# Sums of the left weights bound behind the evictions of block 0's self stage

## The chip, the cores and the metric

The kernel runs on one core of one Trainium2 chip. The metric is device time in microseconds (us) of one execution, as the median of several runs. A profiled execution of the same program gives the trace from which every other duration here is read. Engines: PE is TensorE (PEld its weight loads), DVE is VectorE, ACT is ScalarE, POOL is GpSimd, SP is SyncE; SPq and POOLq are their DMA issues.

## What is computed

Two layers over x (128 sequences of 64 tokens, 768 features, f32), cut here to what matters:

```python
# layer 0
u = h @ h.T / sqrt(d);  p = softmax(u);  attn = (p * adj) / (sum(p * adj) + 1e-10)
h_left, h_self, h_right = h @ W_left.T + b_left, h @ W_self.T + b_self, h @ W_right.T + b_right
ctx = upper(attn) @ h_left + diag(attn) * h_self + lower(attn) @ h_right
x = layernorm(x + relu(layernorm(ctx) * gamma + beta))
# layer 1: 12 heads, scores + beta * adj, masked where adj is 0
x = layernorm(x + softmax(mask(q @ k.T / 8 + beta * adj)) @ v)      # q, k, v = x @ W + b
```

The three weight matrices W_self, W_left and W_right of layer 0 are what this case is about, and of those the work of the first 128 us or so.

## The kernel before, in words

The 8192 tokens are worked in 16 blocks of 512 (four tiles of 128). Every large product of a block, 512 tokens by a 768 x 768 matrix, is made by a scheme with seven products of halves in place of eight (`seven`, L365). For it the weight matrix W is cut into quarters b00, b10, b01, b11 (128 x 1152 each, loaded by SP), and from them four sums are formed on DVE, in this order: t5 = b01 - b00, t6 = b11 - t5, then b01 = b11 - b01 in place (factor 7), and t4 = b10 - t6 (`prepare`, L198; the list of steps is its `later(...)` call). The block's transposed tokens hT are treated in the same way on POOL (`combined`, L312).

`seven` walks the products in the order 1, 2, 6, 5, 7, 4, 3, each for j = 0 and j = 1, that is 14 products of six matmuls (128 x 384). Products 1, 6, 7, 4 add up in one PSUM bank X[j]; 2 and 3 stand in others: 2 in Y[j], then 5 and 3 together in a fresh Y[j]. DVE reads the bank out between them, and PE may go on in it only when DVE has read it:

- after product 1, u1 = X + bias (`first`, L413 to L415)
- after product 2, o = Y + u1 (`last` of `self_part`, L589 to L591), which frees Y for product 5
- after product 6, u2 = X + bias; product 7 for the same j comes on top in X and so waits for that
- after product 7, u3 = X + bias, and o = Y + u3 from what product 5 left; product 4 comes on top in X and waits for u3, and product 3 on top in Y
- after product 4 and after product 3, the last two parts of o.

Block 0 does its self stage (`self_part(0, ...)`, L978), its left stage (L982) and its right stage (L988) with weights that have just been formed in SBUF. Each sum is also stored to DRAM (`store`, L218), so that later blocks stream it. The pieces of the left matrix are asked for by `prepare("l", wst, prep, (2, 1, 0))` at L976: quarters in pieces of 128 x 384 from the pool `wst`, so that each of its sums is three DVE instructions (L234) in place of one; its three new tiles t5, t6, t4 stand in the pool `prep`, which has seven slots, all in use by the self matrix at first. The right matrix's quarters take `prep` slots as those of the self matrix come free, so SP's issues of them wait for PE.

What sets the order: in this part of the program a scheduler lays each engine's instructions in order by its own estimate of when they can start; after that an engine takes them strictly in that order. `prepare` puts the sums in the queue `lazy`, and `step` (L137), called after each product of `seven`, takes from the queues what is due, which settles where they are traced. `tc.issue_after(ins)` adds an ordering edge, with no wait of its own at run time: the instructions traced in its block come after `ins` in the order of the engine of `ins`. `recent["u"]` holds the last DVE eviction that was traced. From block 1's stages on `recent["bound"]` is set (L995) and `step` traces everything behind `recent["u"]`; for block 0 it isn't, and there only the sum 7 of the self matrix is bound (L243).

Of the kernel before, what the change touches and what calls it, by code (L numbers as in the profile page):

```python
# [51 lines left out]
def gnn_two_layers(ctx: ExitStack, tc, x, adj, wl, bl, ws, bs, wr, br, gamma, beta,  # L52
# [52 lines left out]
    for half, sign in ((0, 1), (1, -1)):  # L105
        for g in range(2):
            nc.gpsimd.affine_select(
                out=side[half * L : (half + 1) * L, g, :], in_=side[half * L : (half + 1) * L, g, :],
# [12 lines left out]
    def later(key, *fs, queue=lazy):  # L121
        queue.extend((key, f) if callable(f) else (key, *f) for f in fs)
# [12 lines left out]
    recent = {}  # L135
# [45 lines left out]
    def chunks(pool, name):  # L181


        if pool is not wst:
            tile_ = pool.tile([P, HC, HALF], F32, tag="w", name=name)
            return [tile_[:, k, :] for k in range(HC)], tile_
        return [wst.tile([P, HALF], F32, tag="w", name=name) for _ in range(HC)], None

    def move(queue, whole, parts, to=None, source=None):

        if whole is not None:
            queue.dma_start(out=whole if source is not None else to, in_=source if source is not None else whole)
        else:
            for k in range(HC):
                queue.dma_start(out=parts[k] if source is not None else to[:, k, :],
                                in_=source[:, k, :] if source is not None else parts[k])

    def prepare(nm, quarter_pool, sum_pool, waits=(0, 0, 0), queue=lazy):  # L198

        w = weights[nm].rearrange("(p c) e -> p c e", c=KC)
        src = {(0, 0): w[:, 0:HC, 0:HALF], (0, 1): w[:, 0:HC, HALF:D],
               (1, 0): w[:, HC:KC, 0:HALF], (1, 1): w[:, HC:KC, HALF:D]}
        b = {}
        for q in ((0, 0), (1, 0), (0, 1), (1, 1)):
            b[q] = chunks(quarter_pool, f"b{q[0]}{q[1]}_{nm}")

            with tc.issue_after(streamed["l"][8]) if nm == "k" else ExitStack():
                move(nc.sync, b[q][1], b[q][0], source=src[q])  # L210
        t5, t6, t4 = (chunks(sum_pool, f"t{i}_{nm}") for i in (5, 6, 4))
        in_sbuf = {1: b[0, 0], 2: b[1, 0], 3: b[1, 1], 5: t5, 6: t6, 7: b[0, 1], 4: t4}
        key = ("w", nm)
        if nm in "slrv":
            d = tc.dram_tile([4, P, HC, HALF], F32, name=f"d_{nm}")
            pieces[nm] = {1: src[0, 0], 2: src[1, 0], 3: src[1, 1], 5: d[0], 6: d[1], 7: d[2], 4: d[3]}

        def store(i):  # L218
            if nm in "slrv":
                if i in (5, 6, 7, 4):  # L220
                    move(nc.gpsimd, in_sbuf[i][1], in_sbuf[i][0], to=pieces[nm][i])
            else:


                engine, first = (nc.sync, streamed["s"][20]) if nm == "q" else (nc.gpsimd, last_sum[1].ins)
                with tc.issue_after(first):
                    for hg in range(NHG):
                        engine.dma_start(out=qk_d[hg, i - 1, :, "qk".index(nm)],
                                        in_=in_sbuf[i][1][:, :, hg * P : (hg + 1) * P])

        def formed(i, out, left, right):
            if any(a[1] is None for a in (out, left, right)):
                for k in range(HC):
                    nc.vector.tensor_tensor(out[0][k], left[0][k], right[0][k], ALU.subtract)  # L234
            else:
                nc.vector.tensor_tensor(out[1], left[1], right[1], ALU.subtract)
            store(i)

        def idle():
            pass  # L240

        def formed7():
            with tc.issue_after(evicted["s"].ins) if nm == "s" else ExitStack():  # L243
                formed(7, b[0, 1], b[1, 1], b[0, 1])


        later(key, *[idle] * waits[0], partial(formed, 5, t5, b[0, 1], b[0, 0]),
              *[idle] * waits[1], partial(formed, 6, t6, b[1, 1], t5), formed7,
              *[idle] * waits[2], partial(formed, 4, t4, b[1, 0], t6), queue=queue)
        if nm in "qk":  # L250
            later(key, lambda: store(1), lambda: store(2), lambda: store(3), queue=queue)
        return {i: a[0] for i, a in in_sbuf.items()}
# [771 lines left out]
    for n in range(NBLK):  # L1024
        m, p = n + 1, n - 1
        left, right, own, val = {}, {}, {}, {}
# [174 lines left out]
```

## Time and profile before

| what | value |
|---|---|
| runs shown | 2936.67, 2934.70, 2934.53 us; median 2934.7 |
| profiled execution, its own time | 2938.14 us |
| its span in the trace | 2936.4 us, mean granted PE clock 0.995 |
| PE busy | 2879.9 us, 98% of the span |
| DVE busy | 1989.5 us, 68% |
| ACT, POOL busy | 1123.6 us (38%), 729.9 us (25%) |
| DMA over the span | 210 GB/s |
| block 0's self stage, first to last weight load | 16.19 to 49.36 us |
| block 0's left stage, first weight load | 49.36 us |

In a timeline a row has the start in us, the duration in us, the engine, the line of the kernel, the operation, what it writes and reads, and, in square brackets, how long the engine had sat idle before it and what ended that. A row with x3 stands for three instructions that follow each other. In a table by stretches each row has the bounds of the stretch, its length, the busy time of PE, PEld, DVE, ACT and POOL in it with the number of instructions, the granted PE clock (1.00 is full speed), the DMA share and the rate.

### The profile page before, as it was taken

The page shows a single profiled execution, that of the slowest core. Times are in us where ns is not written, and L with a number is a line of the kernel's source. Part 1 is how long each engine was busy: PE and PEld are TensorE (multiplying, and loading weights), DVE is VectorE, ACT ScalarE, POOL GpSimd, SP SyncE. Part 2 cuts the span into 40 slices and gives each one's busy share as a digit, 9 for nine tenths or more (in the row PEclk, how much of TensorE's full clock was granted, in tenths as well). Part 3 has the DMA queues.
Part 4 walks back from the last instruction along what each step waited for, and adds up shares of the span by engine and source line. Part 5 has one row for each costly group of instructions (what it writes and reads, how often), then busy time and mean ns, then how long its engine had stood idle before and what let it go on. Part 6 is the DMA issues. An engine that isn't in the chain of part 4 may idle for free.

```text
span 2936.4 us, 49944 instructions
## 1 busy us (share of the span) xinstructions
PE 2879.9 (98%) x17578; PEld 1935.1 (66%) x17578; DVE 1989.5 (68%) x4034; ACT 1123.6 (38%) x2114; POOL 729.9 (25%) x879
## 2 busy tenths in 40 slices
PE   8999999999999999999999999999999999999997
PEld 5657567585665856658576575766757567585685
DVE  5678677676676766667667576666767667676656
ACT  0004324354243543434444344443434424354254
POOL 3133122304132130411405124051230413313110
PEclk9999999999999999999999999999999999999998
DMA  9788786849578595775958759486694966849442
GB/s 322 221 274 276 234 233 194 249 138 290 154 197 248 144 285 152 214 231 163 271 147 239 203 175 271 135 260 183 185 260 137 282 163 198 244 139 287 140 127 90
DMA packets 440278, 613.18 MB, mean 209 GB/s; under 512 B 53584, under 2 KB 416720, under 8 KB 440032
## 3 DMA queue, kind: packets, MB, share of 16 engines
q1 hardware_dynamic: 362096, 493.57, 56.0%
q10 hardware_dynamic: 60848, 44.05, 8.2%
q0 software_dynamic: 17088, 72.37, 6.7%
q8 instruction: 143, 2.34, 0.3%
q14 instruction: 103, 0.84, 0.1%
HBM read 539.43 MB, written 77.27 MB: 210 GB/s over the span
## 4 chain that ended last, share of the span: by engine, by line
PE 91%; ACT 3%; POOL 2%; DVE 2%; DMA 1%; issue 1%; SPq 0%; ACTq 0%; DVEq 0%
PE ps_X L384 35%; PE ps_Y L384 26%; PE ps_Y L638 11%; PE ps_X L638 10%; PE ps_ctx L677 3%; ACT eT L853 2%; PE sc L835 2%; PE ps_y L882 2%; PE u L527 2%; POOL q L337 1%; ACT L853 1%; ACT uqk L804 1%; POOL q L336 0%; PE ps_x L286 0%; DVE o L892 0%
## 5 line engine op out<-in xcount | busy, mean ns | idle before, releaser
L384 PE MATMUL ps_X<-xT,wqk 128*128 128x256 f32 x1728 | 395.9, 381 | 9.6 <-ACT uqk L804 9.6
L853 ACT ACTIVATE eT<-s 32x256 f32<-32x256 f32 x768 | 317.8, 414 | 184.7 <-DVE s L862 174.6
L384 PEld LDWEIGHTS ps_X<-xT,wqk 128*128 128x128 f32 x1728 | 325.8, 190 | 67.1 <-ACT uqk L804 16.2
L317 POOL TENSOR_TENSOR S<-hT 128x768 f32<-128x768 f32 x16 | 28.9, 1808 | 1133.4 <-PE ps_Y L384 1102.2
L384 PE MATMUL ps_Y<-S,wqk 128*128 128x256 f32 x1152 | 264.3, 379 | 0.0
L682 ACT ACTIVATE unused<-o 128x768 f32<-128x768 f32 x60 | 50.6, 843 | 500.4 <-DVE o L679 304.9
L384 PEld LDWEIGHTS ps_Y<-S,wqk 128*128 128x128 f32 x1152 | 218.9, 190 | 29.8
L438 DVE TENSOR_TENSOR lr<-ps_Y,u_deep 128x384 f32<-128x384 f32 x273 | 152.1, 557 | 108.6 <-PE ps_Y L638 82.8
L638 PE MATMUL ps_Y<-wlr,q 128*128 128x384 f32 x546 | 208.6, 491 | 0.0
L384 PE MATMUL ps_X<-wv,xT 128*128 128x384 f32 x576 | 195.0, 489 | 0.0
L804 ACT ACTIVATE uqk<-ps_X,bq 128x256 f32<-128x256 f32 x144 | 68.3, 474 | 324.9 <-PE ps_X L384 323.7
L812 DVE TENSOR_TENSOR q<-ps_Y,uqk 128x256 f32<-128x256 f32 x144 | 61.0, 424 | 177.7 <-ACT uqk L804 89.4
L384 PE MATMUL ps_X<-ws,hT 128*128 128x384 f32 x540 | 179.4, 486 | 0.1
L892 DVE SCALAR_TENSOR_TENSOR o<-ps_y,rz,o 128x64 f32<-128x64 f32 x768 | 165.0, 277 | 6.8
L638 PE MATMUL ps_X<-wlr,q 128*128 128x384 f32 x364 | 151.1, 497 | 14.5 <-POOL q L337 5.9
L384 PEld LDWEIGHTS ps_X<-wv,xT 128*128 128x128 f32 x576 | 108.2, 190 | 80.8 <-issue 8.4
L438 DVE TENSOR_TENSOR u_deep<-ps_X,lr 128x384 f32<-128x384 f32 x195 | 107.3, 550 | 68.0 <-PE ps_X L638 66.4
L384 PEld LDWEIGHTS ps_X<-ws,hT 128*128 128x128 f32 x540 | 102.4, 190 | 71.8 <-DMA ws<-in_L_gnn_W_self_dram 0.7
L638 PEld LDWEIGHTS ps_Y<-wlr,q 128*128 128x128 f32 x546 | 101.6, 190 | 67.2
L415 DVE TENSOR_TENSOR u<-ps_X,bv 128x384 f32<-128x384 f32 x96 | 53.4, 556 | 130.3 <-PE ps_X L384 130.2
L384 PE MATMUL ps_X<-S,wqk 128*128 128x256 f32 x576 | 138.2, 385 | 0.0
L384 PE MATMUL ps_Y<-xT,wqk 128*128 128x256 f32 x576 | 135.6, 385 | 0.0
(247 smaller groups left out, 5482.6 us busy)
## 6 DMA issues: line engine op xcount, KB each, us to landing
wlr<-lr_d SPq DMA_DIRECT2D x819, 192.0 KB, 3.5
wqk<-qk_d SPq DMA_DIRECT2D x672, 192.0 KB, 2.4
wv<-d_v SPq DMA_DIRECT2D x192, 192.0 KB, 3.3
ws<-d_s SPq DMA_DIRECT2D x180, 192.0 KB, 6.0
wv<-in_L_gnn_Wv_dram SPq DMA_DIRECT2D x144, 192.0 KB, 4.1
ws<-in_L_gnn_W_self_dram SPq DMA_DIRECT2D x135, 192.0 KB, 5.5
xa<-in_x_dram SPq DMA_DIRECT2D x64, 384.0 KB, 5.4
out_dram<-o POOLq DMA_DIRECT2D x62, 384.0 KB, 6.2
```

The costliest lines, as they stand in the source:

```text
L384: nc.tensor.matmul(ps, lhsT=a, rhs=b, start=(c == 0 and i in (1, 2, 5)), stop=(c == len(fs) - 1), skip_group_check=True)
L415: recent["u"] = evicted[nm] = nc.vector.tensor_tensor(u, ps, bias[nm][:, b * HALF : (b + 1) * HALF], ALU.add)
L438: nc.vector.tensor_tensor(dst, view(ps), add, ALU.add)
L527: nc.tensor.matmul(u[g * L : (g + 1) * L, t, :], lhsT=xT[:, c, tok], rhs=xT[:, c, tok], start=(c == 0), stop=(c == KC - 1))
L638: nc.tensor.matmul(ps, lhsT=a, rhs=b, start=(k == 0 and j in (1, 2, 5)), stop=(k == len(fs) - 1), skip_group_check=True)
L677: nc.tensor.matmul(ps[g * L : (g + 1) * L, 0:HALF], lhsT=blk["aT"][:, t, g * L : (g + 1) * L], rhs=blk["lr"][t][:, g, cols], start=True, s ...
L804: nc.scalar.activation(u, ps, AF.Identity, bias=bias["qk"[j]][:, c : c + 1])
L812: nc.vector.tensor_tensor(dst, ps, part, ALU.add)
L835: nc.tensor.matmul(sc[r][g * L : (g + 1) * L, t, c, :], lhsT=q[rows, c, tok], rhs=k[rows, c, tok], start=True, stop=True)
L853: nc.scalar.activation(e[cols, :, rows], pairs[rows, :, cols], AF.Exp)
L882: nc.tensor.matmul(y[r, h][cols, t, c, :], lhsT=eT[rows, 2 * h + t, c, cols], rhs=v[rows, 2 * h + t, g, hg + c * HC, :], start=True, stop= ...
L892: nc.vector.scalar_tensor_tensor(res[:, r, c, hg, :], ps[:, t, k, 0:HD], rz[:, t, k : k + 1], res[:, r, c, hg, :], ALU.mult, ALU.add)
```

## The change

The DVE subtractions of `formed` move into a function `subtracted`, and for the left matrix alone they are traced behind the eviction that was traced last. The store stays outside the bound block. The self, right and layer 1 matrices are traced as before.

```diff
         def formed(i, out, left, right):
+
+            with tc.issue_after(recent["u"].ins) if nm == "l" else ExitStack():
+                subtracted(out, left, right)
+            store(i)
+
+        def subtracted(out, left, right):
             if any(a[1] is None for a in (out, left, right)):
                 for k in range(HC):
                     nc.vector.tensor_tensor(out[0][k], left[0][k], right[0][k], ALU.subtract)
             else:
                 nc.vector.tensor_tensor(out[1], left[1], right[1], ALU.subtract)
-            store(i)
```

Lines of the kernel below L239 stand five lines further down in the changed kernel.

In the built programs, DVE's order between the eviction of product 6, j = 0, and the first evictions of the left stage goes from this (evictions named by their product; t and b are the left sums)

```
before: ev6/0  t5 t5 t5 t6  ev6/1  t6 t6 b b b t4 t4 t4  ev7/0 o  ev7/1 o  ev4/0  ev4/1  ev3/0  (t_r)  ev3/1
after:  ev6/0  ev6/1  ev7/0 o  ev7/1 o  t5 t5 t5  ev4/0  ev4/1  t6 t6 t6  ev3/0  b b b  ev3/1  t4 t4 t4
```

and the right sums (t_r) move behind the left stage's evictions of products 1 and 2. PE's, ACT's and POOL's orders are the same in both. In SP's order the first load of a quarter of W_right moves behind two small loads (bv, adj), and the first two loads for W_v move ahead of some of the six loads of W_self for block 1; from the load of d_s on it is the same.

## The prediction

> **What bounds the kernel now.** I read the busy shares and the slices of the page first. PE is busy for 98% of the span, so elsewhere an edit on DVE is worth nothing; what can be won lies where PE stands or is slow.
>
> ```profile
> PE 2879.9 (98%) x17578; PEld 1935.1 (66%) x17578; DVE 1989.5 (68%) x4034; ACT 1123.6 (38%) x2114; POOL 729.9 (25%) x879
> PE   8999999999999999999999999999999999999997
> ```
>
> Then PE's waits. One DVE eviction (L415) costs PE 2.9 us in one piece, the second longest PE wait in the list; the longest, 5.5 us, is the load of x at the start.
>
> ```profile
> PE ps_x L286 <- DMA xa<-in_x_dram: 6.8, 2, 5.5
> PE ps_X L384 <- DVE u L415: 2.9, 1, 2.9
> ```
>
> The timeline places it in block 0's self stage. I read it against the products: the PE row at 31.78 is product 7 (both j), the one at 38.82 is product 4, the one at 45.81 product 3, the one at 49.68 product 1 of the left stage.
>
> ```profile
> 29.25 0.55 DVE L415 TENSOR_TENSOR u<-ps_X,bs 128x384 f32<-128x384 f32 x1
> 29.72 1.49 DVE L234 TENSOR_TENSOR t_l<-b_l 128x384 f32<-128x384 f32 x3
> 31.78 4.14 PE L384 MATMUL ps_X<-b_s,hT 128*128 128x384 f32 x12
> 32.63 0.56 DVE L234 TENSOR_TENSOR t_l<-b_l,t_l 128x384 f32<-128x384 f32 x1 [1.43 <-DMA b_l<-in_L_gnn_W_left_dram]
> 33.11 0.55 DVE L415 TENSOR_TENSOR u<-ps_X,bs 128x384 f32<-128x384 f32 x1
> 34.46 1.03 DVE L234 TENSOR_TENSOR t_l<-b_l,t_l 128x384 f32<-128x384 f32 x2 [0.80 <-DMA b_l<-in_L_gnn_W_left_dram]
> 35.40 1.49 DVE L234 TENSOR_TENSOR b_l<-b_l 128x384 f32<-128x384 f32 x3
> 36.81 1.49 DVE L234 TENSOR_TENSOR t_l<-b_l,t_l 128x384 f32<-128x384 f32 x3
> 38.22 0.55 DVE L415 TENSOR_TENSOR u<-ps_X,bs 128x384 f32<-128x384 f32 x1
> 38.82 7.16 PE L384 MATMUL ps_X<-t_s,hT 128*128 128x384 f32 x12 [2.90 <-DVE u L415]
> 45.81 4.03 PE L384 MATMUL ps_Y<-b_s,S 128*128 128x384 f32 x12
> 49.68 4.03 PE L384 MATMUL ps_X<-b_l,hT 128*128 128x384 f32 x12
> ```
>
> Twelve sums of left weights stand in DVE's queue ahead of the eviction of product 7 (38.22), two of them waiting for loads of W_left. Product 7, j = 0, had ended near 33.7, so its eviction is over 4 us late, and PE stands. And then product 4 takes 7.16 us where every other such row takes 4.03. The table by stretches of 3.41 us (the clock is the third number from the end) shows why:
>
> ```profile
> 34.72:38.13 3.41, 1.20 (x4) 0.38 (x2) 3.41 (x8) 0.00 (x0) 2.14 (x4) 1.00 0.96 370
> 38.13:41.54 3.41, 2.72 (x5) 1.51 (x6) 2.21 (x5) 0.00 (x0) 0.54 (x1) 0.50 1.01 362
> 41.54:44.96 3.42, 3.42 (x7) 1.91 (x6) 0.56 (x1) 0.00 (x0) 0.00 (x0) 0.50 1.04 412
> 44.96:48.37 3.41, 3.41 (x11) 1.98 (x11) 0.98 (x2) 0.00 (x0) 1.48 (x2) 1.00 1.05 377
> ```
>
> The clock is halved from 38.13 to 44.96.
>
> **What the Trainium skill says.** "TensorE: Matmul & The Clock Gate", Part 1 (The HAM clock gate): the PE clock goes to half after an idle window of about 3413 ns and back after a busy one, and the windows run free, not from the kernel's start. The trace agrees: 44.96 - 38.13 = 6.83 us is two such windows. It adds that a window need not be all idle: that from 34.72 was 35% busy (1.20 of 3.41) and halved the clock, and the next, 80% busy, did not restore it. "Perfetto Trace Analysis", Tensor Engine Instruction: DVE takes its queue strictly in order; the trace agrees, the eviction at 38.22 starts as the last sum ends.
>
> **The change, part by part.**
>
> 1. *The two late evictions are freed.* No instruction is added or removed; the ordering edge is inside one engine and waits for nothing at run time. By the changed order DVE goes from the eviction at 29.25 straight to that of product 6, j = 1 (29.72 to 30.3; its product ended near 27.9). Product 7, j = 1, thus no longer waits, and PE keeps its pace of 3.87 us per product (weight loads start at 23.72, 27.59, 31.46). Product 7, j = 0, starts at 31.78 and ends at 33.7; DVE starts about 0.2 us later (the trace: product 3 starts at 45.81, takes 1.94 for j = 0, evicted at 47.95), so 33.9, done 34.5. Product 4 needs this at 31.78 + 3.87 = 35.65: 1.2 us early. Then o (35.06), and product 7, j = 1: 35.86 to 36.4, needed at 37.6.
>
> 2. *The stall goes*: product 4 at 35.65 in place of 38.82, that is 3.17 us.
>
> 3. *The slow clock goes with it*: product 4 took 45.81 - 38.82 = 6.99 us of PE's time where 3.87 is its pace, 3.12 us. Without an idle window it isn't slowed. Sum in the profiled execution: 6.29 us, the left stage's first weight load from 49.36 to 31.46 + 3 x 3.87 = 43.07.
>
> 4. *The sums in their new place.* t5 after the two o: 37.0 to 38.4 (three at 0.47 each); the loads that DVE waited for had landed by 34.46. Evictions of product 4 at 38.4 and 39.7; t6 40.3 to 41.7; eviction of product 3 to 42.2; b to 43.6; eviction to 44.15; t4 to 45.6. Left product 1 ends its j = 0 at 45.3, so its eviction (45.6 to 46.1) starts just behind the last sum, five us before product 6 needs it. Left product 6 needs t6 at 43.4 + 2 x 3.87 = 51.1: nine us in hand. Cost nothing, hidden by products 4 and 3 of the self stage; were the sums nine us later, PE would stand in the left stage instead.
>
> 5. *The right sums* follow the left stage's evictions of products 2. SP issues the quarters of W_right as prep slots come free: the third at 46.01 and the fourth at 49.88 now, as products 4 and 3 end; then at about 39.6 and 43.5. The third landed by 52.73, 6.7 us after issue; the rows of these loads go from 4.3 to 14.9 us. DVE reaches the first right sum at about 50.4; behind it queue the evictions of product 2, j = 1 (PE needs it at 57) and of product 6. At 6.7 us the load lands at 46.3, at 10 us at 49.6: no wait; at 14.9 us at 54.5, still before 57. Cost nothing.
>
> 6. *Other queues.* POOL's order is the same; its stores of the left sums start some us later (t5 31.50 now, about 38.4 then) and nobody on PE's path waits for them before block 1. On SP the first load for W_v waits for the slot of t6 (end of left product 6, about 55) and now stands ahead of loads of W_self for block 1, which come at 53.75 now; these are used from 116.15, 60 us later. Cost nothing. Bounds: 0 to +1 us.
>
> 7. *After the left stage* PE's chain has no wait on anything at a fixed time until product 1 of block 1's self stage at 116.15: all its weight loads there follow each other at 3.87. A shift there passes to the end. A wait on DVE before 328.11 halves the clock for one more window (328.26 to 331.67); its phase against the free windows changes, which can cost or give up to about 1.7 us in one run, nothing on average.
>
> **From the profiled run to the runs shown.** Its own time is 2938.14, and the sum there is 2938.14 - 6.29 = 2931.85. The runs shown are 1.5 to 3.6 us shorter, median 2934.7, so they may have paid less for the same stall. Where the free windows fall decides: sliding a window of 3.41 us over the 2.90 us gap, with the clock lost below half busy and regained only in a full window, the penalty is one window at half speed, 3.41 / 2 = 1.7 us, in about half of the positions, near 3 us in a quarter, nothing in 15 to 30%. (The threshold is an estimate: the trace has a window 43% busy that halved the clock and one 61% busy, from 2905.3, that didn't.) The trace's 3.12 is thus near the top. Likeliest for a median: 3.17 + 1.7 = 4.9 us, 2934.7 - 4.9 = 2929.8. Bounds: above, 6.3 us, 2928.4. Below: of the stall 2.2 us are DVE's waits for W_left, which may be shorter unprofiled. Without them the eviction at 38.22 starts at 36.0, product 4 at 36.6, and the stall is 0.9 us, perhaps with the clock kept: 2933.8.
>
> **Rivals.**
>
> - *The full sum* (6.3 us, 2928.4; 5.9 us and more): the runs shown paid as the profiled one. For it, the trace; against it, that the profiled run is the slowest of all. Chance 0.34.
> - *A small stall outside the profile* (under 3.5 us, 2931.2 to 2933.8). For it, 2.2 us of load waits on DVE with the DMA share near 1; against it, six us of sums stand in front of the eviction in any case. Chance 0.15.
> - *Slower*: the right sums take over. If the third quarter of W_right lands after 57, DVE stands with the eviction of left product 2 behind it, and product 5 with it; each us later is a us, plus up to 3.4 us of half clock. To end slower than before it must eat 4.9 us first, so land after about 60.2 (57 + 4.9 - 1.7), and for 0.2% slower after about 66: 26 us after issue against 14.9 at most now. Time then 2941. Chance 0.03.
> - *The order doesn't move as said*: the built order shows it moved. No chance of its own.
>
> The likeliest case, 3.5 to 5.9 us, has 0.48 and its own range 2928.8 to 2931.2.
>
> **Chances.** 0.2% is 5.9 us, about what a measurement of this kernel can tell from no change; it lies inside my gain's range. Faster by more: 0.34; within: 0.48 + 0.15 = 0.63; slower: 0.03. The range leaves out the lowest gains, the slower case and a little beyond the full sum: 2928.0 to 2932.4.
>
> **What would show it.** PE without a gap between 16.2 and 104, product 4 at 35.7 with a duration of 4.03 and the clock at 1.00 from 38 to 45, the left stage's first weight load near 43.1, the sums t5 after two o. Wrong would be a DVE wait on W_right above 5 us with PE standing in the left stage, or the gain lost again between 320 and 335.

## The result, and the profile after

| | before | after |
|---|---|---|
| median of 15 runs each, same chip | 2936.67 us (2934.53 to 2939.71) | 2930.33 us (2928.96 to 2934.45) |
| profiled execution, its own time | 2938.14 us | 2930.10 us |
| its span, mean granted PE clock | 2936.4 us, 0.995 | 2928.4 us, 0.997 |

The ratio after to before is 0.9981, 95% interval 0.9974 to 0.9988: faster by 5.6 us (3.5 to 7.6). The forecast was 2929.8, a gain of 4.9 us from a median of 2934.7.

The busy shares and PE's slices on the page of the changed kernel:

```profile
PE 2875.6 (98%) x17578; PEld 1933.5 (66%) x17578; DVE 1990.3 (68%) x4034; ACT 1123.3 (38%) x2114; POOL 728.6 (25%) x879
PE   9999999999999999999999999999999999999997
```

The counts are the same and DVE's busy time differs by 0.8 us: nothing was saved on DVE. PE's first slice, 8 before, is 9. Among PE's waits the load of x is still the longest single one (5.1 us); the wait for the eviction u (2.9 us before) has no line any more:

```profile
PE ps_x L291 <- DMA xa<-in_x_dram: 5.7, 2, 5.1
```

The timeline of the changed kernel over the same part of block 0 follows (lines lie five or six further down: L384, L415, L591 and L234 of before are L389, L420, L596 and L240). A matmul of this f32 kernel stands as two records in the trace: the x6 of a product for one j are three matmuls, the x12 of a row both j. PE's rows are, as before, product 7 (31.53), product 4, product 3, and product 1 of the left stage:

```profile
28.96 1.01 DVE L420 TENSOR_TENSOR u<-ps_X,bs 128x384 f32<-128x384 f32 x2
31.53 4.03 PE L389 MATMUL ps_X<-b_s,hT 128*128 128x384 f32 x12
33.67 0.56 DVE L420 TENSOR_TENSOR u<-ps_X,bs 128x384 f32<-128x384 f32 x1 [3.69 <-PE ps_X L389]
34.26 0.56 DVE L596 TENSOR_TENSOR o<-ps_Y,u 128x384 f32<-128x384 f32 x1
35.40 4.03 PE L389 MATMUL ps_X<-t_s,hT 128*128 128x384 f32 x12
35.60 0.56 DVE L420 TENSOR_TENSOR u<-ps_X,bs 128x384 f32<-128x384 f32 x1 [0.79 <-PE ps_X L389]
36.67 1.49 DVE L240 TENSOR_TENSOR t_l<-b_l 128x384 f32<-128x384 f32 x3
39.27 4.03 PE L389 MATMUL ps_Y<-b_s,S 128*128 128x384 f32 x12
43.14 4.03 PE L389 MATMUL ps_X<-b_l,hT 128*128 128x384 f32 x12
```

The reader sees the roles exchanged. Before, PE waited for DVE; now DVE stands idle for 3.69 us and is woken by PE, so the eviction of product 7, j = 0, runs at 33.67 as its product ends, and product 4 starts 3.87 us after product 7. The first three left sums follow the second o, at 36.67. In the table by stretches the clock (third number from the end) is at full speed where it was 0.50, and PE is busy throughout:

```profile
34.87:38.29 3.42, 3.42 (x12) 1.98 (x11) 2.65 (x6) 0.00 (x0) 0.00 (x0) 1.00 1.02 293
38.29:41.70 3.41, 3.41 (x12) 2.07 (x11) 2.56 (x6) 0.00 (x0) 0.53 (x1) 1.00 1.05 361
41.70:45.11 3.41, 3.41 (x12) 1.95 (x12) 3.41 (x8) 0.00 (x0) 2.14 (x4) 1.00 1.07 406
```

**Where the 8.0 us between the two profiled executions lie.** Product 7's row starts at 31.53 in place of 31.78: 0.25 us, an earlier start of PE and not the change. The left stage's first row starts at 43.14 in place of 49.68, that is 6.54 us earlier, of which 6.29 lie between product 7 and here: the stall and the slow clock. In block 2 a row at 328.11 has become one at 321.55 (6.56 earlier), but two rows on, 332.40 has become 324.22, and the shift is 8.2. PE's rows there, of the kernel before and then of the changed one (`eT` is made by DVE, which PE waits for in both):

```profile
328.11 1.06 PE L882 MATMUL ps_y<-v,eT 64*64 64x65 f32 x32 [1.18 <-DVE eT L857]
329.10 3.46 PE L384 MATMUL ps_Y<-wl,S 128*128 128x384 f32 x6
332.40 4.03 PE L384 MATMUL ps_X<-wr,hT 128*128 128x384 f32 x12
```

```profile
321.55 0.70 PE L887 MATMUL ps_y<-v,eT 64*64 64x65 f32 x32 [1.18 <-DVE eT L862]
322.18 2.20 PE L389 MATMUL ps_Y<-wl,S 128*128 128x384 f32 x6
324.22 4.03 PE L389 MATMUL ps_X<-wr,hT 128*128 128x384 f32 x12
```

The same wait of 1.18 us halved the clock in one trace (3.46 us for six records) and not in the other (2.20). That is 1.6 us of the 8.0, and it is chance and not the change, as the runs below show: of the thirteen traces of this case twelve have these two PE waits (0.75 and 1.18), and the clock was lost behind them in four (the kernel before and three of the experiments) and kept in eight (the changed kernel's two, two variants of the kernel before and four others).

### The profile page after: what moved, and what is told of

It reads as the page before. It is cut to its first block, busy times and chain, and to the rows that moved or that the text cites. A ratio compares the mean times of both kernels' runs of the same rounds, so it can differ in the third digit from the quotient of the medians.

```text
span 2928.4 us, 49941 instructions
## 1 busy us (share of the span) xinstructions
PE 2875.6 (98%) x17578; PEld 1933.5 (66%) x17578; DVE 1990.3 (68%) x4034; ACT 1123.3 (38%) x2114; POOL 728.6 (25%) x879
## 4 chain that ended last, share of the span: by engine, by line
PE 93%; ACT 3%; POOL 2%; DVE 1%; issue 1%; DMA 0%; SPq 0%; DVEq 0%; ACTq 0%
PE ps_X L389 36%; PE ps_Y L389 27%; PE ps_Y L643 11%; PE ps_X L643 10%; PE ps_ctx L682 3%; ACT eT L858 2%; PE sc L840 2%; PE ps_y L887 2%; PE u L532 2%; POOL q L342 1%; ACT L858 1%; ACT uqk L809 1%; PE ps_x L291 0%; POOL q L341 0%; DVE o L897 0%
## 5 line engine op out<-in xcount | busy, mean ns | idle before, releaser
L389 PE MATMUL ps_X<-xT,wqk 128*128 128x256 f32 x1728 | 395.8, 381 | 9.5 <-ACT uqk L809 9.5
L389 PEld LDWEIGHTS ps_X<-xT,wqk 128*128 128x128 f32 x1728 | 325.8, 190 | 67.0 <-ACT uqk L809 16.2
L389 PE MATMUL ps_Y<-S,wqk 128*128 128x256 f32 x1152 | 264.3, 379 | 0.0
L389 PEld LDWEIGHTS ps_Y<-S,wqk 128*128 128x128 f32 x1152 | 218.9, 190 | 29.8
L389 PE MATMUL ps_X<-wv,xT 128*128 128x384 f32 x576 | 195.0, 489 | 0.0
L389 PE MATMUL ps_X<-ws,hT 128*128 128x384 f32 x540 | 179.2, 486 | 0.0
L389 PEld LDWEIGHTS ps_X<-wv,xT 128*128 128x128 f32 x576 | 108.1, 190 | 80.8 <-issue 8.4
L389 PEld LDWEIGHTS ps_X<-ws,hT 128*128 128x128 f32 x540 | 102.5, 190 | 71.4
L420 DVE TENSOR_TENSOR u<-ps_X,bv 128x384 f32<-128x384 f32 x96 | 53.5, 557 | 130.2 <-PE ps_X L389 130.2
L389 PE MATMUL ps_X<-S,wqk 128*128 128x256 f32 x576 | 138.1, 385 | 0.0
L389 PE MATMUL ps_Y<-xT,wqk 128*128 128x256 f32 x576 | 135.6, 385 | 0.0
```

The lines of the kernel that those rows point to most:

```text
L389: nc.tensor.matmul(ps, lhsT=a, rhs=b, start=(c == 0 and i in (1, 2, 5)), stop=(c == len(fs) - 1), skip_group_check=True)
L420: recent["u"] = evicted[nm] = nc.vector.tensor_tensor(u, ps, bias[nm][:, b * HALF : (b + 1) * HALF], ALU.add)
```

## The experiments

The theory: the left sums ahead of product 7's eviction make PE stand, and the gap then halves its clock; the new order removes both. Its rivals: the slow clock is all of it or none of it in the runs outside the profile; the waits for W_left's loads are the cause and an earlier load does the same; the gain comes from something else that the order moved. Three groups of kernels were run, each with its own runs of the kernel before: the two halves of the change, the earlier loads and the fillers in the kernel before (2935.97, median of 49 runs); the changed kernel again and the delays (2935.8 of 57); the two further kernels with earlier loads and the heads of block 2 (2936.18 of 44). Each kernel is compared within its group unless it is said otherwise. Where an interval of a difference of medians is given, it comes from resampling the runs.

**The changed kernel again.** No edit.

> The changed kernel itself once more, as the yardstick for the three runs beside it, which all start from it. Expected: 5.5 to 6.5 us faster than before, no PE gap in block 0's self stage. Its left stage begins three product pairs (11.6 us) after product 7; in before the same point hangs on W_left's last load (about 33 us in both traces of this part), so the gain should be larger the earlier PE starts.

2930.62 us (21 runs), ratio 0.9983 (0.9977 to 0.9990): by medians 5.18 us faster than before. PE has no wait in the self stage. The delays further down are compared with this median. In this trace DVE waits longer for W_right than in the first one (0.83 us, to 51.10):

```profile
51.93 0.56 DVE L240 TENSOR_TENSOR t_r<-b_r 128x384 f32<-128x384 f32 x1 [1.98 <-DMA b_r<-in_L_gnn_W_right_dram]
```

PE still keeps its pace of 3.87 us per row (twelve records) through the left stage.

**Half of the change: products 7 and 4's sums alone bound** (b and t4; t5 and t6 are left to the scheduler).

```diff
-            with tc.issue_after(recent["u"].ins) if nm == "l" else ExitStack():
+            with tc.issue_after(recent["u"].ins) if nm == "l" and i in (7, 4) else ExitStack():
```

> One part of the change alone: only the later two sums of the left matrix (factor 7 in place, and t4) are traced behind the last eviction; t5 and t6 stay in front of the evictions of product 6, j = 1, and product 7, with their two load waits. Theory: the eviction of product 6, j = 1, is as late as before (33.1), so product 7, j = 1, starts at 33.7; the eviction of product 7 at 35.4, product 4 near 36.0, stall about 0.4 us, the clock kept: about 5.5 to 6 us faster than before in the profile, nearly the whole change. Rival: the load waits in front of product 6's eviction are what costs, then less than half of the gain is left (below 3 us).

2932.49 us (13 runs), ratio 0.9989 (0.9981 to 0.9997): 3.5 us faster by medians, where 5.5 to 6 were expected. DVE's and PE's rows of its timeline:

```profile
32.30 0.56 DVE L240 TENSOR_TENSOR t_l<-b_l 128x384 f32<-128x384 f32 x1 [1.36 <-DMA b_l<-in_L_gnn_W_left_dram]
33.99 0.55 DVE L420 TENSOR_TENSOR u<-ps_X,bs 128x384 f32<-128x384 f32 x1
34.60 3.90 PE L389 MATMUL ps_X<-b_s,hT 128*128 128x384 f32 x6 [2.25 <-DVE u L420]
```

The six sums that stayed ahead wait for loads (1.36 us here, 3.13 in all). In this execution PE had begun its self stage at 14.44 us (16.19 in the profile of before), and the loads land no earlier for that. So product 7, j = 1, stands for 2.25 us, for the eviction of product 6, and runs at half speed (3.90 us for six records where 2.10 is usual, 1.80 more). Half of the sums are removed, and the stall stands one eviction earlier. That place goes with PE's early start: the kernel before stands there too when PE begins at 13.95 us (the run with fillers, below). This execution, 2935.38 us, is the second slowest of the thirteen, so most of them lost less than its trace.

**The other half: products 5 and 6's sums alone bound** (t5 and t6).

```diff
-            with tc.issue_after(recent["u"].ins) if nm == "l" else ExitStack():
+            with tc.issue_after(recent["u"].ins) if nm == "l" and i in (5, 6) else ExitStack():
```

> The other part alone: only t5 and t6 of the left matrix are bound; factor 7 and t4 are free. By the built order all twelve sums then come after both evictions of product 7, only the sums of factor 7 come a little sooner than in the changed kernel. Theory: no stall, PE as in the changed kernel, the same time as that within 1 us, some 5 to 6.5 us faster than before. Rival: a sum ahead of product 4's second eviction holds up the left stage, then up to 1 us of PE wait at the left stage's first product.

2930.26 us (21 runs), ratio 0.9982 (0.9975 to 0.9988): all of the gain, 5.7 us by medians. In its trace all twelve sums stand behind both evictions of product 7, and PE doesn't stand:

```profile
34.30 4.03 PE L389 MATMUL ps_X<-t_s,hT 128*128 128x384 f32 x12
34.50 0.56 DVE L420 TENSOR_TENSOR u<-ps_X,bs 128x384 f32<-128x384 f32 x1 [0.79 <-PE ps_X L389]
35.57 1.48 DVE L240 TENSOR_TENSOR t_l<-b_l 128x384 f32<-128x384 f32 x3
```

Binding these six sums, the ones that wait for the loads, is thus enough. It doesn't show what they cost alone, for the other six went behind them: b is overwritten only when t5 has read it, and t4 reads t6.

**The loads earlier instead of the sums later**: the kernel before, with W_left asked for ahead of the rows of block 1.

```diff
+    in_sbuf_l = prepare("l", wst, prep, (2, 1, 0))
     rows = sq_p.tile([P, T, D], F32, tag="sq", name="rows")
...
-    in_sbuf_l = prepare("l", wst, prep, (2, 1, 0))
```

> The kernel before, with the loads of W_left asked for ahead of those of block 1's rows, about 4 us earlier; no sum is bound, and by the built order all twelve left sums still stand in front of the eviction of product 7. It parts the stall into waits for loads (2.2 us) and queued sums. Theory that the loads were a part of it: no DVE wait on W_left, product 4 near 36.6, stall about 0.9 us, the clock kept, 4 to 5.5 us faster than before. Rival that the order of the queue alone decides: product 4 still near 38.8 and the time of before, within 1 us.

2937.86 us (13 runs), ratio 1.0005 (0.9997 to 1.0013): not faster, by medians 1.9 us slower, where 4 to 5.5 us faster was expected. The timeline shows why:

```profile
34.76 4.14 PE L384 MATMUL ps_X<-t_s,hT 128*128 128x384 f32 x12 [0.48 <-DVE u L415]
51.82 0.56 DVE L234 TENSOR_TENSOR t_r<-b_r 128x384 f32<-128x384 f32 x1 [10.39 <-DMA b_r<-in_L_gnn_W_right_dram]
52.30 0.55 DVE L591 TENSOR_TENSOR o<-ps_Y,u 128x384 f32<-128x384 f32 x1
52.90 3.47 PE L384 MATMUL ps_Y<-b_l,hT 128*128 128x384 f32 x6 [4.33 <-DVE o L591]
56.16 4.50 PE L384 MATMUL ps_X<-t_l,S 128*128 128x384 f32 x12
60.50 4.03 PE L384 MATMUL ps_Y<-t_l,S 128*128 128x384 f32 x12
```

The stall of the self stage shrinks to 0.48 us (0.9 was expected), and the clock is kept there. Then DVE, in its order of before, comes early to the first right sum, waits 10.39 us for a load of W_right, and the last eviction of the self stage (52.30) stands behind it: PE stands for 4.33 us and loses its clock (60.50 - 52.90 = 7.60 us for 18 records, where 5.80 is the pace: 1.80 us). It is the same fault, one matrix on. It is also the mechanism of the prediction's slower rival, in a kernel in which it can occur.

**The same loads with the change** (the changed kernel, W_left asked for first as above).

> The changed kernel with the loads of W_left ahead of those of block 1's rows. In the kernel before, that order of loads took the stall out of the self stage (0.5 us left) and put one of 6.4 us into the left stage, where DVE waited 10.4 us for W_right with an eviction of product 3 queued behind. In the changed kernel the right sums come behind the left stage's first eviction of product 2. Theory: W_right lands as late (near 52), DVE waits a few us for it, but PE needs the eviction behind it only at 56; no stall, the changed kernel's time within 1 us, over 5 us faster than before. Rival: the late W_right costs here too, 3 us or more.

2930.49 us (21 runs), ratio 0.9982 (0.9976 to 0.9989): as the changed kernel. In its trace PE began late (16.80 us), so the first right sum hardly waited (0.1 us):

```profile
51.22 0.56 DVE L240 TENSOR_TENSOR t_r<-b_r 128x384 f32<-128x384 f32 x1
```

So this trace doesn't show a late W_right under the new order. The times alone say that the earlier loads cost nothing there; the longest wait for W_right that a trace shows under the new order is the 1.98 us of the changed kernel's second one, and PE didn't stand for it.

**The right sums bound in place of the left**, W_left asked for first.

```diff
-            with tc.issue_after(recent["u"].ins) if nm == "l" else ExitStack():
+            with tc.issue_after(recent["u"].ins) if nm == "r" else ExitStack():
```

> The loads of W_left ahead of those of block 1's rows, and the sums of the right matrix bound behind the last eviction in place of those of the left one, which stand where they stood before. If what matters is only that no sum whose load is late stands ahead of an eviction that PE needs, then this does about as much as the change: the left sums cost about 1.2 us in the self stage (as seen with these loads in the kernel before), no stall in the left stage: 1 to 1.5 us slower than the changed kernel, 4 to 5 us faster than before. Rival: binding the left sums is needed, then no more than 2 us faster than before.

2931.33 us (21 runs), ratio 0.9984 (0.9977 to 0.9990): 0.84 us behind the kernel above, 4.85 ahead of before. PE waits 0.48 us in the self stage and nowhere in the left one:

```profile
34.73 4.14 PE L389 MATMUL ps_X<-t_s,hT 128*128 128x384 f32 x12 [0.48 <-DVE u L420]
```

This is the missing half of the experiment with the earlier loads: they are worth nearly the whole gain, once the right sums stand behind the evictions. The twelve left sums ahead of product 7's eviction, without their waits, cost PE 0.48 us; with the earlier loads DVE begins them at 25.72 us, where it began at 29.72 in the kernel before.

**The stall put back without the sums, with late evictions**: the changed kernel, and 14 additions of the bias ahead of the evictions of product 7. Their results are written over by that eviction.

```diff
+            with tc.issue_after(recent["u"].ins) if late and kept is False and b else ExitStack():
+                for _ in range(late if (j, b, kept) == (0, 1, False) else 0):
+                    nc.vector.tensor_tensor(u, bias[nm][:, 0:HALF], bias[nm][:, 0:HALF], ALU.add)
...
+        by_tokens("s", blk["S"], last, in_sbuf, hooks, 14 if n == 0 else 0)
```

(The transposes into `ps_a` of block 0 are also bound behind the last matmul, so that PE's order stays.)

> The changed kernel with a stall of known cause put back: 14 DVE additions of 128x384 (their result is overwritten) between the evictions of product 6 and that of product 7, j = 0, and no load in it. 0.47 to 0.59 us each, so product 4 starts 2.3 to 4 us late. Theory of two costs: the time added is the stall plus the half clock behind it, 1.7 to 3.1 us for it in most executions, so 4 to 6.5 us slower than the changed kernel, near the kernel before. Rival, the clock loss belongs to the loads or is an artefact of the trace: only the stall itself, 2.3 to 4 us.

2936.09 us (13 runs), ratio 1.0001 (0.9993 to 1.0009): the time of before, 5.47 us over the changed kernel (4.6 to 7.0). The timeline, and a stretch from the time at half clock, which lasts from about 37.7 to 44.4 us:

```profile
30.03 8.26 DVE L422 TENSOR_TENSOR u<-bs 128x384 f32<-128x384 f32 x14
39.00 6.80 PE L389 MATMUL ps_X<-t_s,hT 128*128 128x384 f32 x12 [3.51 <-DVE u L423]
45.64 4.03 PE L389 MATMUL ps_Y<-b_s,S 128*128 128x384 f32 x12
```

```profile
38.20:41.60 3.40, 2.60 (x4) 1.51 (x5) 3.23 (x8) 0.00 (x0) 0.00 (x0) 0.50 1.04 357
```

Product 4 was due at 35.32 in this execution, so the stall is 3.68 us; it then takes 6.64 us of PE's time where 3.87 is its pace, 2.77 more. A late eviction of about the size that the sums made (3.17 us in the profile of before) gives the time that they cost. If the stall of the other executions is that of this trace, the clock's part in the times is 5.47 - 3.68 = 1.8 us.

**A shorter delay**: 11 additions in place of 14.

> The changed kernel with 11 such additions: product 4 starts 0.9 to 2.2 us late, below or near half a clock window of 3.41 us. Theory: the clock is kept or seldom lost, so 1 to 2.5 us slower than the changed kernel and no more. Rival: any PE gap costs the clock, then 3 to 5 us.

2932.91 us (21 runs), ratio 0.9991 (0.9984 to 0.9997): 2.29 us over the changed kernel (1.5 to 3.7).

```profile
36.72 4.14 PE L389 MATMUL ps_X<-t_s,hT 128*128 128x384 f32 x12 [2.11 <-DVE u L423]
40.69 4.04 PE L389 MATMUL ps_Y<-b_s,S 128*128 128x384 f32 x12
```

The stall is 2.27 us (36.72 where 34.45 was due), the clock stays at full speed (40.69 - 36.72 = 3.97), and the time is the stall's alone. 1.4 us less of stall took 3.2 us off the time. The length of the gap alone doesn't decide it: 2.11 us kept the clock here, and 2.25 us lost it in the trace of the first half of the change.

**The delay with PE kept busy**: 14 additions again, and four matmuls (x8 in the trace) into a spare bank between products 7 and 4. `kept` holds the operands of the product before; the result isn't used.

```diff
+                if filler and (i, j) == (4, 0):
+                    spare = ps_mm.tile([P, 512], F32, tag="mm", name="spare")
+                    for c in range(filler):
+                        a, b = kept[c % len(kept)]
+                        nc.tensor.matmul(spare[:, 0:width], lhsT=a, rhs=b, start=True, stop=True)
```

> As the run before (14 DVE additions ahead of product 7's eviction), with four extra matmuls, 2.6 us, between products 7 and 4, their result unused. The eviction is as late, but PE stands for 1.4 us at most. Theory: product 4 takes 4.0 us at full clock; the difference to the run without the matmuls is the clock term alone, 1.5 to 3 us faster than it. Rival: no difference.

2934.64 us (13 runs), ratio 0.9996 (0.9988 to 1.0004): 4.02 us over the changed kernel, 1.45 us (0.1 to 2.9) under the delay without fillers.

```profile
35.76 2.74 PE L392 MATMUL spare<-b_s,hT 128*128 128x384 f32 x8
38.70 4.14 PE L395 MATMUL ps_X<-t_s,hT 128*128 128x384 f32 x12 [0.19 <-DVE u L429]
```

Product 4 is as late as the delay makes it (2.94 us behind 35.76), PE stands only 0.19 us of it, and it runs at its pace: the delay without the slow clock. The clock's share in the times is thus about 1.5 us by this pair, and 1.8 by the run without fillers; the interval is wide. Of the 4.02 us the trace explains 2.94, the late eviction. Where the other 1.1 us come from isn't shown; the stall may be longer in executions in which PE begins earlier than here (16.30 us), as it is in the trace without fillers (3.68 us, begun at 15.87).

**The kernel before with the same fillers.**

> The kernel before, with four extra matmuls (128x384, about 0.65 us each by the trace, their result unused) between products 7 and 4 of block 0's self stage. They fill 2.6 us of the 2.9 us for which PE stands there; the eviction that product 4 waits for is as late as before. Theory: the stall has two costs, the standing (3.2 us) and the half clock that follows (3.1 us in the profiled run of before, about 1.7 in a typical one). Then product 4 still starts near 38.8, but takes 4.0 us in place of 7.2 and the clock stays at 1.00: 1.7 to 3.1 us faster than before. Rival: the slow product 4 has another cause (weights or DMA traffic near 400 GB/s); then it still takes about 7 us, and the time is that of before.

2936.33 us (13 runs), ratio 1.0000 (0.9992 to 1.0008): nothing won, where 1.7 to 3.1 us were expected. The trace shows that the fillers missed the gap:

```profile
13.95 4.14 PE L390 MATMUL ps_X<-b_s,hT 128*128 128x384 f32 x12
34.77 3.09 PE L390 MATMUL ps_X<-b_s,hT 128*128 128x384 f32 x6 [2.90 <-DVE u L421]
37.65 3.59 PE L387 MATMUL spare<-b_s,hT 128*128 128x384 f32 x8
41.08 4.03 PE L390 MATMUL ps_X<-t_s,hT 128*128 128x384 f32 x12
```

In this execution PE had begun at 13.95 us, and so it stood one product earlier, ahead of product 7, j = 1; the fillers came to a clock already slow (41.08 - 34.77 = 6.31 us for 14 records, where 4.51 is the pace: 1.80 us). They cost time as well: the eviction that product 4 needs was done at 39.02, but behind the fillers product 4 starts at 41.08. As far as this trace goes, the run is thus no test of the clock's term. It does show that where PE stands is not fixed: DVE's waits for W_left add up to 3.66 us here and to 2.2 in the profile of before, in which PE began at 16.19.

**The two waits of block 2 taken away**: the changed kernel, with the last heads of block 0, and the finishing of that block, traced two products later (in the branch `m < DEEP`, which block 0 alone takes).

```diff
-                at(left, 13, weighted, p, 2)
-                at(right, 0, finish_by_act, p)
+                at(right, 1, weighted, p, 2)
+                at(right, 2, finish_by_act, p)
```

> The changed kernel, with the last weighted heads of block 0 traced two products of the right stage later (and the finishing of block 0 two later), as the later blocks have it. In both traces PE stands there twice for DVE's transposes of the exponentials (0.75 and 1.18 us near 320 us), which in the trace of before cost the clock as well (3.46 in place of 2.20 us). Theory: both waits vanish, 1.9 us for them and 0 to 1.7 for the clock: 2 to 3 us faster than the changed kernel, near 2928. Rival: the transposes are late by more than two products, or another eviction is next in line; then under 1 us.

2928.60 us (8 runs), ratio 0.9973 (0.9963 to 0.9984): 1.9 us (1.2 to 3.9) under the changed kernel with W_left asked for first, which ran in the same group; 2 to 3 us were expected against the changed kernel.

```profile
320.78 2.10 PE L389 MATMUL ps_X<-wr,hT 128*128 128x384 f32 x6
322.81 1.16 PE L887 MATMUL ps_y<-v,eT 64*64 64x65 f32 x64
323.90 2.20 PE L389 MATMUL ps_X<-wr,hT 128*128 128x384 f32 x6
```

The two heads follow each other without a wait, and the waits that go (0.75 + 1.18 = 1.93 us) are of the size of the difference. Eight runs don't tell whether a part of the clock went with them.

## Why the prediction was right

Its mechanism held in the traces at every step but for one landing time, and the time of 2929.8 is 0.5 us from what came. By its steps:

1. *The two late evictions are freed.* Right: 33.67 for the forecast 33.9, product 7, j = 1's at 35.60 for 35.86, each about 0.25 us early, as PE had begun earlier by that.
2. *The stall goes, 3.17 us.* Right: product 4 starts 35.40 - 31.53 = 3.87 us after product 7 (7.04 before). The 14 additions, which make the eviction late without the sums, put the time back (5.47 us), so nothing else that the order moved is needed to explain it.
3. *The slow clock goes, 3.12 us in the profiled run.* Right for that run: the self stage, from its first row to the left stage's first, takes 43.14 - 15.95 = 27.19 us where it took 49.68 - 16.19 = 33.49: 6.30, for a sum of 6.29. Outside the profile the prediction took one window at half speed, 1.7 us; the delays give 1.5 (0.1 to 2.9) and 1.8. The traces agree with its argument from the sliding of the free windows over the gap: behind a long wait of PE's the slow clock took 1.80 us in three of them (the half with b and t4 bound, the earlier loads and the fillers in the kernel before), 2.77 and 3.12 in two (the 14 additions, the kernel before), and nothing in one (the 11 additions). The profile's 3.12 is thus the largest. For the kernel before, the split of the gain into stall and clock outside the profile isn't measured: the stall varies with PE's start. The full-sum rival (6.3 us; 5.9 and more) is less likely, not excluded: by medians the repeated run gains 5.2 and the half with t5 and t6 bound 5.7, but the result gains 6.3, with an interval by the ratio of 3.5 to 7.6.
4. *The left sums cost nothing in their new place.* Right: t5 starts at 36.67, and PE has no wait to the end of the left stage.
5. *The right sums cost nothing.* Right for PE, with one detail wrong: for "no wait" DVE had 0.83 us of idle time, to 51.10 (1.98 us, to 51.93, in the second trace). The load of the third quarter was issued at 39.47, near the forecast 39.6, but took about 11.5 us to land, where "no wait" rested on 6.7 to 10 (its bound of 14.9 was not reached); DVE had the time in hand. A W_right later than that was not tried under the new order: in the kernel meant to do so PE began late.
6. *Other queues, 0 to +1 us.* No cost appeared.
7. *The shift passes to the end.* Right: 6.56 us at the row of block 2 named, and the phase of the window there gave 1.6 us more, in this pair of executions, within the 1.7 allowed.

Two terms were off in size. *The base*: the median of three runs, 2934.7, lies 1 to 2 us below every later median of the same kernel (2936.67 of 15 runs, 2935.8 to 2936.18 of 44 to 57). *The gain*: 4.9 us forecast, 5.6 by the ratio, 5.2 and 6.3 by medians. The two errors are of opposite effect on the time, so the closeness of 2929.8 is partly luck. And one bound looked for the waits in the wrong place: "of the stall 2.2 us are DVE's waits for W_left, which may be shorter unprofiled". What the traces show is that they grow the earlier PE begins: 2.23 us for 16.19, 3.13 for 14.44, 3.66 for 13.95. Unprofiled waits can't be read. The small-stall rival (under 3.5 us) rested on that bound; the gains of the changed kernel by medians, 5.2 and 6.3, lie above it.

That the slow clock can come of less than an idle window of 3.4 us is what the sum needed. The Trainium skill, "TensorE: Matmul & The Clock Gate", Part 1 (HAM oscillation), has the rule "no PE-idle gaps >~3.4µs". The traces differ, and decide: 2.90 us of idle time halved the clock for 6.83 us in the kernel before, 2.25 us did so in the trace of the first half of the change, and 1.18 us behind a wait of 0.75 did in four traces of twelve.

Still open: how the spread between executions divides between PE's start and the phase of the windows. PE began anywhere between 13.95 and 16.80 us in the traces, and no run controlled it.

## What to carry to other kernels

DVE took its queue in order here, so that each of its waits was passed on to all that stood behind it: put work that waits for a load, or is wanted much later, behind the evictions that PE waits for now, and look for the next such place before you move a load earlier, since the wait moves with it. Price a gap of about 3 us on PE at its length plus something like half a window of 3.4 us; that is an estimate from the traces and delays here (1.5 to 1.8 us, with a wide interval), and one profile may show nearly twice that (3.12 us) or, at 2.11 us of gap, nothing. Before you take a few tenths of a per cent from a median, have more than three runs behind it.

## What the runs showed of the hardware

- Behind a window of 3.41 us that was 35% busy (from 34.72 in the kernel before) the clock was halved, behind one 61% busy (from 2905.30) it wasn't; the same two waits of 0.75 and 1.18 us halved it in four traces out of twelve.
- Single gaps of 2.25, 2.90 and 4.33 us cost 1.80 us each by the slow clock, 2.90 and 3.51 in two other traces 3.12 and 2.77, and one of 2.11 us nothing: two gaps of the same 2.90 us cost 1.80 and 3.12.
- Fourteen additions that write the same tile follow each other at 0.59 us (8.26 / 14); sums to different tiles at 0.47 (1.49 for three, the last 0.56 long).
- PE's first product starts between 13.95 and 16.80 us in these traces, of kernels whose programs differ little up to there.
